# Two transformer layers in one kernel: the order of attention products over TensorE's row groups, and the key sums of the last queries

## The chip, the cores and the metric

The kernel runs on one core of one Trainium2 chip. The metric is the device time of one execution, in microseconds: the median of several runs. A profile of one further execution gives the engines' instructions with their starts and lengths. The profile calls the engines PE (TensorE's products) and PEld (its weight loads), DVE (VectorE), ACT (ScalarE), POOL (GpSimd) and SP (which issues DMAs).

## The reference

Two layers work on x of shape (2, 2048, 256), 16 heads. Each layer normalises x and adds the product of two branches, `x + s * g`.

```python
xn = _layernorm(x)
s = _L0_attn_ref(xn, ...)            # linear attention
g = _silu(_L0_ffn_ref(xn, ...))      # a transformer block: causal softmax attention
x = x + s * g                        #   with 16 channels a head, then 8 experts, top 2
xn = _layernorm(x)
s = _L1_attn_ref(xn, ...)            # causal softmax attention, real and imaginary parts,
g = _silu(_L1_ffn_ref(xn, ...))      #   together 32 channels a head; int4 weights, LoRA
x = x + s * g
```

What matters here are the two causal softmax attentions, each over 2048 queries and keys, 2 batches and 16 heads:

```python
scores = jnp.where(causal, q @ k.T * scale, -big)
probs = jax.nn.softmax(scores, -1)
out = probs @ v
```

## The kernel before

**Three parts.** Attention 1 (of the first layer's block, with the linear attention, the norms and the routing dealt in between), the experts, and attention 2 (with the second layer's other branch in between). Both attentions are built by one function, `run_attention` (L550), which runs over 2 batches x 4 groups of four heads. The four heads of a group lie on partitions 0 to 31, 32 to 63, 64 to 95 and 96 to 127, so each head's products use one row group of TensorE's array, 32 rows high and 128 columns wide, and products of four heads can stand in the array side by side. This is called the row shape below. The products of weights with values use the column shape (128 rows, 32 columns a head), and everything else the whole array.

**Two passes.** Pass A (`pass_a`, L568) takes 128 queries against up to 512 keys and forms scores (L575), with queries on the partitions; DVE takes their maximum (L594), which is later subtracted from the queries. In attention 1 a diagonal piece gets the causal mask by four small bf16 products a head, of 128, 96, 64 and 32 columns (`hide`, L529, product at L534); in attention 2 DVE adds the mask and takes the maximum (L588). Pass B (`pass_b`, L601) takes 256 queries against a pair of key tiles with keys on the partitions: two products of 256 columns a head (L609; on the diagonal one of 256 and one of 128), in attention 2 one or two three-row bf16 products that bring in the maximum (`less_maximum`, L1691, products at L1697, L1698 and L1700), and on the diagonal four mask products (`hide_pair`, L536, product at L541). ACT then takes the exponential (L621) into `pt`. One turn `u` of the loop in `run_attention` makes a **unit**: pass A for one piece and pass B for one pair, four heads each.

**Banks.** Scores go to PSUM, which is eight banks of 512 fp32 columns a partition. Pass A takes two neighbouring banks for two heads, since one DVE instruction reduces both; pass B takes one bank a head. A full unit thus takes two pairs and four single banks, all eight.

**Sums of the weights.** In attention 2 POOL adds the weights `pt` over the key tiles of two pairs into `ps` (L1717, L1721, L1722), and a product with ones sums `ps` over the partitions (L1751); the products with values are L1740. For the last 256 queries of the last group, POOL leaves out the last pairs (`direct`, L1725: `p >= c - 1`, c = 7) and products of `pt` itself with ones give the sums (L1747).

**What orders the work.** Nothing is issued as the functions run: each calls `S = plan.step`, which notes a step with its strand (S for scores and sums, A and B for the passes' DVE and ACT work, prep, lin, mix, gate, end and others), engine, cost, reads, writes, and for TensorE where it stands (`on`: a row group's number, "col" or "all"). A planner (`Plan.run` and `Plan.advance`, L223) then searches for the order, with a beam and random handicaps, under a model of time that has queues, banks and buffers; within one strand and engine the order of the calls is kept. Steps of the strands prep, lin, mix and gate may not come before `plan.pace`. In the model before, a product in row shape begins when its group is free and the queue behind it goes on 0.01 us later, whatever group comes next:

```python
if t > groups[s.on] or st.cold[s.on]:
    t += s.load
...
done, free["PE"] = t + s.cost + self.TAIL - self.GAP, sent + 0.01
```

A step on TensorE is one product of pass A, or both products of pass B, or all four masks of a head, or the maximum's products of a head. In a unit their order is, with A0 for pass A of head 0 and so on: A0, B2, A1, B3, the masks and late maxima of these four, then A2, B0, A3, B1 and theirs.

Of the kernel before, what the change touches and what calls it, by code (L numbers as in the profile page):

```python
# [17 lines left out]
P = 128  # L18
# [76 lines left out]
class State:  # L95


    def __init__(self, plan):
        self.main = next(iter(plan.queues.get(("S", "PE"), ())), None)
        self.can = {k: q[0] for k, q in plan.queues.items() if not q[0].before}  # L100
        self.waits = [s.before + (s is not plan.queues[s.key][0]) for s in plan.steps]
        self.ready = [0.0] * len(plan.steps)
        self.slot = [None] * len(plan.bufs)
        self.left = [b.uses for b in plan.bufs]
        self.until = [0.0] * len(plan.bufs)
        self.guest = [None] * len(plan.bufs)
        self.since = {k: [0.0] * (plan.BANKS if k == "s" else len(x)) for k, x in plan.kinds.items()}
        self.free, self.groups, self.cold = {}, [0.0] * 4, [True] * 4
        self.mode, self.used, self.held = None, 0.0, {}
        self.todo, self.done, self.value = len(plan.steps), [], 0.0  # L110
# [10 lines left out]
class Plan:  # L121
# [101 lines left out]
    def advance(self, st, handicaps, until):  # L223

        free, groups, can, ready = st.free, st.groups, st.can, st.ready
        while st.todo:
# [4 lines left out]
            for key, s in can.items():  # L231
# [6 lines left out]
                if eng == "PE":  # L238
                    closed = strand != "S" and not (gap and st.used + s.cost <= self.LIMIT)
                    x = top if s.kind != st.mode else groups[s.on] if s.row else top - self.MODE  # L240
                    if x > busy:
                        busy = x
# [43 lines left out]
            if s.eng == "PE":  # L286
                st.used = st.used + s.cost if key[0] != "S" else 0.0
                kind = s.kind
                if kind != st.mode:
                    if kind == "row":  # L290
                        groups[:] = [max(t, x) for x in groups]
                    st.cold[:] = [True] * 4
                if s.row:
                    if t > groups[s.on] or st.cold[s.on]:
                        t += s.load
                    st.cold[s.on] = False
                elif t > max(groups) or st.cold[0]:
                    t += s.load
                    st.cold[0] = False
                done, free["PE"] = t + s.cost + self.TAIL - self.GAP, sent + 0.01  # L300
                if kind == "row":
                    st.mode, groups[s.on] = "row", t + s.cost
                    worth /= 4
                else:
                    st.mode, groups[:] = s.on, [t + s.cost] * 4
            elif s.eng == "SP":
                free["SP"] = t + 0.06
# [70 lines left out]
def kernel(ctx: ExitStack, tc: tile.TileContext, i: dict, out: bass.AP):  # L378
# [81 lines left out]
    def t_row(n):  # L460
        return 0.00167 * n
# [65 lines left out]
    T_HIDE_A, T_HIDE_B = 0.15, 0.28  # L527

    def hide(out, j, mask):  # L529

        r = slice(32 * j, 32 * j + 32)
        for q in range(4):
            cols = slice(32 * q, P)
            nc.tensor.matmul(out[:, cols], ident_h[r, q], mask[r, q, cols], start=False, stop=q == 3)  # L534

    def hide_pair(out, j, mask):  # L536

        r, v = slice(32 * j, 32 * j + 32), out.rearrange("p (n k) -> p n k", n=2)
        for q in (3, 2, 1, 0):
            cols = slice(0, 32 * q + 32)  # L540
            nc.tensor.matmul(v[:, :, cols], ident_h[r, q], mask[r, q, :, cols], start=False, stop=q == 0)  # L541
# [8 lines left out]
    def run_attention(plan, make, prepare, subtract, sum_keys, finish, last_sum, before=None, others=(), between=False, causal=None):  # L550
# [17 lines left out]
        def pass_a(g, t, k, i, w, mx, parts):  # L568
# [11 lines left out]
            def products(x):  # L580
                return S("S", "PE", t_row(w), lambda: score(x), r=[(g.qt, t), *((g.kt, n) for n in keys)], w=[(s, x)], on=i + x)

            def rest():
                for x in range(2) if diagonal and causal is None else ():
                    S("S", "PE", T_HIDE_A, lambda x=x: hide(s.t[:, x, w - P : w], i + x, mask_q), r=[(s, x), "ident_h", "mask_q"], w=[(s, x)], on=i + x)
# [15 lines left out]
        def pass_b(g, c, p, j, pt):  # L601
# [5 lines left out]
            def score():  # L607
                for n, (kj, q0, at) in enumerate(halves_of(c, p)):
                    nc.tensor.matmul(  # L609
                        s.t[:, at], g.kt.t[r, kj * P : (kj + 1) * P], g.qt.t[r, QC * c + q0 : QC * (c + 1)],  # L610
                        start=n == 0 and not ahead, stop=n == 1 and not (diagonal or before and not ahead),
                    )

            def rest():
                if before and not ahead:
                    S("S", "PE", 0.25 * t_row(w), before(g, c, j, s, diagonal, False, not diagonal), r=[s, g.mh[c]], w=[s], on=j, load=0.026)
                if diagonal:
                    S("S", "PE", T_HIDE_B, lambda: hide_pair(s.t[:, : 2 * P], j, mask_h), r=[s, "mask_h"], w=[s], on=j)
# [4 lines left out]
            reads = [(g.kt, 2 * p), (g.kt, 2 * p + 1), (g.qt, 2 * c), (g.qt, 2 * c + 1)]  # L623
            opener = None
            if ahead:
                opener = S("S", "PE", 0.25 * t_row(w), before(g, c, j, s, diagonal, True, False), r=[g.mh[c]], w=[s], on=j, load=0.026)
                reads.append(s)
            step = S("S", "PE", t_row(w), score, r=reads, w=[s], on=j)
            return opener or step, rest, weigh
# [4 lines left out]
        for u in range(at + last_sum + 1):  # L634
# [10 lines left out]
            first = None  # L645
            for i in (0, 2):


                more = []
                if a:  # L650
                    products, after_a = pass_a(g, t, k, i, wa, mx, parts)
                for x in range(2):
                    if a:
                        plan.pace = products(x)
                        first = first or plan.pace
                    if b:
                        step, rest, weigh = pass_b(gb, cb, p, (i + 2 + x) % 4, pt)
                        first = first or step
                        more.append((rest, weigh))
                if a:  # L660
                    after_a()
                for rest, _ in more:
                    rest()
                for _, weigh in more:
                    weigh()
# [848 lines left out]
    with ExitStack() as sc:  # L1514
# [176 lines left out]
        def less_maximum(G, c, j, s, diagonal, first, last):  # L1691
            r = slice(32 * j, 32 * j + 3)

            def product():
                m = G.mh[c].t[r]
                if diagonal:
                    nc.tensor.matmul(s.t[:, :P], ones_h[r], m[:, P:], start=first, stop=False)  # L1697
                    nc.tensor.matmul(s.t[:, P : P + QC], ones_h[r], m, start=False, stop=last)  # L1698
                else:
                    nc.tensor.matmul(  # L1700
                        s.t.rearrange("p (n q) -> p n q", n=2), ones_h[r], m[:, None].to_broadcast([3, 2, QC]),
                        start=first, stop=last,
                    )

            return product

        def sum_keys(G, c, pair, last):
# [17 lines left out]
            direct = G.b == B - 1 and G.g == NG - 1 and c == NT // 2 - 1 and p >= c - 1  # L1725
# [156 lines left out]
```

## Time and profile before

| | |
|---|---|
| median of 3 runs | 3334.01 us (3331.4 to 3335.59) |
| the profiled execution | 3333.86 us, its span 3332.1 us, granted TensorE clock 0.982 |
| PE, DVE, ACT, POOL busy | 96%, 64%, 49%, 49% of the span |
| attention 1, experts, attention 2 | 0 to 1374, 1374 to 1909, 1909 to 3332 us |
| L575, products of pass A | 5120 passes, 1282.3 us busy |
| L609, products of pass B | 9216 passes, 1239.8 us busy |
| L621, exponential on ACT | 2304 of 577 ns mean |
| L594, maximum on DVE | 1024 of 1122 ns mean |

An fp32 product shows as two passes, each with a weight load of its own, so 5120 passes are 2560 products. Busy time of PE is the time in which at least one product is in the array; products of different row groups lie over each other in it. Some records of products are missing from a trace. The timeline of an engine gives start, length, line, tiles, shapes and count, and merges neighbours of one line and shape, which then show with the length of all together; idle time and what ended it stand in brackets.

### The profile page before, as it was taken

Reading aid. Unit: us, or ns where it says so; the run is one execution under the profiler, and the core shown is the slowest. Engines: PE = TensorE matmul, PEld = TensorE weight load, DVE = VectorE, ACT = ScalarE, POOL = GpSimd, SP = SyncE. Lnnn points to the kernel's source line nnn. Section 1 sums busy time; section 2 is a strip of 40 time slices with the busy share of each in tenths; the row PEclk is TensorE's granted clock in tenths of the full one; section 3 lists DMA queues with packets and bytes.
Section 4 is the critical chain, followed back from the end, with each engine's and each line's share of the span. In section 5 each row is a group of like instructions: output and inputs, shape, how many; then the busy total and the mean of one; then the engine's idle time right before and its main releaser. Section 6 shows DMA issues by size and latency. Waiting matters only on the chain.

```text
span 3332.1 us, 92022 instructions
## 1 busy us (share of the span) xinstructions
PE 3205.3 (96%) x39748; PEld 2271.7 (68%) x39748; DVE 2132.9 (64%) x4250; ACT 1623.4 (49%) x3264; POOL 1620.8 (49%) x2006
## 2 busy tenths in 40 slices
PE   7999999989999999979999989999999999999998
PEld 5677777767777776656666646666766666767775
DVE  5677677667777767641112057787777776777785
ACT  3565555555555555511112155555554555544554
POOL 5442222333233222310000057898987776878887
PEclk9999999999999999989999989999999999999999
DMA  5000000000000010133342131110101001000000
GB/s 198 2 2 2 5 8 8 17 30 26 6 11 5 9 45 13 49 109 115 109 131 94 64 105 43 38 43 29 39 17 33 27 17 40 23 12 23 14 29 24
DMA packets 99742, 134.51 MB, mean 40 GB/s; under 512 B 9461, under 2 KB 76739, under 8 KB 99334
## 3 DMA queue, kind: packets, MB, share of 16 engines
q1 hardware_dynamic: 93190, 114.74, 10.6%
q0 software_dynamic: 6144, 13.88, 1.3%
q8 instruction: 311, 5.10, 0.6%
q14 instruction: 97, 0.79, 0.1%
HBM read 93.75 MB, written 37.75 MB: 39 GB/s over the span
## 4 chain that ended last, share of the span: by engine, by line
PE 50%; DVE 3%; POOL 2%; ACT 1%; issue 1%; DMA 0%; POOLq 0%; another core or an unknown queue 0%; SPq 0%; DVEq 0%; ACTq 0%
PE banks L575 9%; PE banks L609 8%; PE banks L414 8%; PE banks L1740 7%; PE s L1488 7%; PE s L1494 7%; PE banks L1751 2%; PE banks L1700 1%; PE banks L541 1%; PE banks L1698 1%; DVE mx L594 1%; POOL ps L1721 1%; ACT pt L621 1%; POOL ps L1717 0%; POOL ps L1722 0%
## 5 line engine op out<-in xcount | busy, mean ns | idle before, releaser
L621 ACT ACTIVATE pt<-banks 128x512 f32<-128x512 f32 (+1 forms) x2304 | 1160.7, 577 | 721.9 <-PE banks L609 321.3
L594 DVE TENSOR_REDUCE mx<-banks 128x2 f32<-128x1024 f32 (+3 forms) x1024 | 1119.1, 1122 | 337.4 <-PE banks L609 141.7
L575 PE MATMUL banks<-carried,carried 32*128 32x512 f32 (+3 forms) x5120 | 1282.3, 566 | 25.0 <-DVE mx L594 10.5
L609 PE MATMUL banks<-carried,carried 32*128 32x256 f32 (+1 forms) x9216 | 1239.8, 378 | 3.8 <-issue 3.7
L609 PEld LDWEIGHTS banks<-carried,carried 32*128 32x128 f32 x9216 | 972.1, 186 | 42.8 <-issue 15.8
L575 PEld LDWEIGHTS banks<-carried,carried 32*128 32x128 f32 x5120 | 545.3, 185 | 242.3 <-issue 108.6
L1717 POOL TENSOR_TENSOR ps<-pt 128x1024 f32<-128x1024 f32 (+1 forms) x159 | 346.7, 2181 | 113.8 <-ACT pt L621 101.8
L1721 POOL TENSOR_TENSOR ps<-ps,pt 128x1024 f32<-128x1024 f32 x127 | 302.4, 2381 | 69.3 <-ACT pt L621 64.8
L848 POOL TENSOR_TENSOR ra<-raw,rope 128x128 f32<-128x128 f32 x128 | 60.1, 470 | 566.3 <-ACT raw L860 496.1
L1700 PE MATMUL banks<-mh,ones_h 3*128 3x512 bf16 x896 | 272.0, 382 | 7.5 <-ACT mh L1688 3.5
L1722 POOL TENSOR_TENSOR ps<-ps,pt 128x1024 f32<-128x1024 f32 (+1 forms) x127 | 269.1, 2119 | 10.0
L911 PE MATMUL banks<-pt,vt 128*32 128x256 f32 (+1 forms) x4608 | 269.1, 371 | 4.3 <-DVE mx L594 3.0
L1740 PE MATMUL banks<-pt,vt 128*32 128x256 f32 (+1 forms) x4608 | 269.0, 371 | 2.5 <-ACT pt L621 2.5
L1497 DVE TENSOR_TENSOR ye<-s,b 128x256 f32<-128x256 f32 x64 | 27.2, 424 | 380.6 <-PE s L1494 380.6
L588 DVE CUSTOM_DVE_ANT_0 banks<-banks,causal 128x384 f32<-128x384 f32 (+3 forms) x512 | 240.3, 515 | 40.5 <-PE banks L575 25.2
L1489 ACT ACTIVATE hm<-s,b1c 128x512 f32<-128x512 f32 x128 | 87.8, 687 | 347.2 <-PE s L1488 346.0
L1488 PE MATMUL s<-xt,carried 128*128 128x512 f32 x512 | 228.2, 604 | 9.7 <-DVE xt L1421 9.7
L1494 PE MATMUL s<-carried,hm 128*128 128x256 f32 x1024 | 223.6, 379 | 0.0
L1740 PEld LDWEIGHTS banks<-pt,vt 128*32 128x32 f32 x4608 | 135.2, 110 | 129.5 <-ACT pt L621 26.4
L1494 PEld LDWEIGHTS s<-carried,hm 128*128 128x128 f32 x1024 | 194.6, 190 | 33.3 <-issue 7.7
L911 PEld LDWEIGHTS banks<-pt,vt 128*32 128x32 f32 x4608 | 134.0, 109 | 114.4 <-issue 15.7
L1488 PEld LDWEIGHTS s<-xt,carried 128*128 128x128 f32 x512 | 97.4, 193 | 131.2 <-issue 110.2
(276 smaller groups left out, 4166.9 us busy)
## 6 DMA issues: line engine op xcount, KB each, us to landing
carried<-in_L_ffn_W_dram SPq DMA_DIRECT2D x32, 1024.0 KB
gl<-g_dram SPq DMA_DIRECT2D x64, 256.0 KB
slots_in<-zero SPq DMA_DIRECT2D x8, 1024.0 KB
slots_out<-ye SPq DMA_DIRECT2D x16, 512.0 KB
xe<-slots_in SPq DMA_DIRECT2D x15, 512.0 KB
s_dram<-lo SPq DMA_DIRECT2D x16, 256.0 KB
hn<-in_L_attn_x_dram SPq DMA_DIRECT2D x16, 256.0 KB
g_dram<-gs SPq DMA_DIRECT2D x16, 256.0 KB
```

What stands on the lines that cost most here:

```text
L575: nc.tensor.matmul(s.t[:, x, :w], g.qt.t[r, t * P : (t + 1) * P], g.kt.t[r, 512 * k : 512 * k + w], start=True, stop=not (diagonal and cau ...
L594: S("A", "DVE", t_dve(2 * w), lambda: nc.vector.tensor_reduce(mx.t[:, t % 2, i : i + 2, k], s.t[:, :, :w], AX.X, ALU.max), r=[(s, 0), (s, ...
L609: nc.tensor.matmul(s.t[:, at], g.kt.t[r, kj * P : (kj + 1) * P], g.qt.t[r, QC * c + q0 : QC * (c + 1)], start=n == 0 and not ahead, stop=n ...
L621: S("B", "ACT", t_act(w), lambda: nc.scalar.activation(pt.t[:, j, :w], s.t[:, :w], AF.Exp, scale=0.25), r=[s], w=[(pt, j)])
L911: nc.tensor.matmul(av.t[32 * j : 32 * j + 32, q0:QC], vts[G.vn][:, kj, j], pt.t[:, j, at], start=n == 0, stop=n == len(tiles) - 1,)
L1488: nc.tensor.matmul(ps, w1[:, k, f * P : (f + 1) * P], xt[:, k], start=k == 0, stop=k == 1)
L1494: nc.tensor.matmul(ps[:, :D], hm[:, f, s * P : (s + 1) * P], w2[:, f], start=f == 0, stop=f == FF // P - 1)
L1700: nc.tensor.matmul(s.t.rearrange("p (n q) -> p n q", n=2), ones_h[r], m[:, None].to_broadcast([3, 2, QC]), start=first, stop=last,)
L1717: nc.gpsimd.tensor_tensor(ps.t[:, :, q0:], pt.t[:, :, same], pt.t[:, :, odd], ALU.add)
L1721: nc.gpsimd.tensor_tensor(ps.t, ps.t, pt.t[:, :, even], ALU.add)
L1722: nc.gpsimd.tensor_tensor(ps.t[:, :, q0:], ps.t[:, :, q0:], pt.t[:, :, odd], ALU.add)
L1740: nc.tensor.matmul(av.t[32 * j : 32 * j + 32, q0:QC], G.vt.t[:, kj, j], pt.t[:, j, at], start=n == 0, stop=False)
```

## The change

The planner's model is changed: a product in row shape is sent only when the product before it in its group has begun, and what stands behind it in TensorE's queue waits with it. A change of shape waits until all groups are done.

```diff
+                    if s.row and s.kind == st.mode and began[s.on] > t:
+                        t = busy = began[s.on]
...
+                if s.kind != st.mode:
+                    sent = max(sent, max(groups) + self.MODE)
+                    st.mode, groups[:], began[:] = s.kind, [sent] * 4, [sent] * 4
                 if s.row:
-                    if t > groups[s.on] or st.cold[s.on]:
-                        t += s.load
-                    st.cold[s.on] = False
...
+                    t = max(groups[s.on], sent + s.load)
+                    began[s.on], groups[s.on] = t, t + s.cost
                     worth /= 4
                 else:
-                    st.mode, groups[:] = s.on, [t + s.cost] * 4
+                    t = max(groups[0], sent + s.load)
+                    began[:], groups[:] = [t] * 4, [t + s.cost] * 4
+                done, free["PE"] = t + s.cost + self.TAIL - self.GAP, sent + 0.007
```

Each single product is a step of its own: `hide`, `hide_pair` and `less_maximum` return lists of products with their costs, and `hide` and `hide_pair` now give the narrowest mask first. In attention 1 (`before` is None) the steps of a unit are dealt out: each group's products stand in their order, and the four lists are merged by the time at which the product ahead in the group would begin. In attention 2 they are sorted by half and phase, which is the order of before.

```diff
-                        step, rest, weigh = pass_b(gb, cb, p, (i + 2 + x) % 4, pt)
...
+            order = []
+            for j, q in enumerate(queues):
+                began, until = -1.0, 0.0
+                for n, entry in enumerate(q):
+                    order.append((began, j, n, entry))
+                    began, until = until, until + entry[0]
+            order.sort(key=lambda x: x[:3])
+            if before:
+                order = [(0, j, 0, entry) for _, j, entry in sorted(by_step, key=lambda x: x[0])]
+            for _, j, _, (cost, fn, r, w_, load, *_) in order:
+                step = S("S", "PE", cost, fn, r=r, w=w_, on=j, load=load)
+                first = first or step
+            if a:
+                plan.pace = step
```

`plan.pace` is now the last row product of a unit, where it was the last product of pass A. Last, the sums of the last 256 queries of the last group are all made by products with ones, none by POOL:

```diff
-            direct = G.b == B - 1 and G.g == NG - 1 and c == NT // 2 - 1 and p >= c - 1
+            direct = G.b == B - 1 and G.g == NG - 1 and c == NT // 2 - 1
```

The instructions themselves stay the same in number and size, but for 48 more products with ones of `pt` and 12 fewer of `ps`, and nine fewer adds on POOL; the order on every engine is planned anew. Line numbers shift by up to 16: pass A's product stays L575, pass B's is L610, the masks are L527 and L537, the maximum's products L1711, L1719 and L1720, the products with values L1756, and those with ones L1767 and L1763.

## The prediction

> **What bounds the kernel now.** I read the shares of the engines first, then the three parts of the program as windows, then TensorE's own timeline inside one unit of attention, and the end last.
>
> ```profile
> PE 3205.3 (96%) x39748; PEld 2271.7 (68%) x39748; DVE 2132.9 (64%) x4250; ACT 1623.4 (49%) x3264; POOL 1620.8 (49%) x2006
> ...
> 0.00:1374.00 1374.00, 1324.47 (x16740) 978.94 (x16740) 971.94 (x1811) 764.58 (x1628) 450.27 (x1086) 0.99 0.07 24
> 1374.00:1909.00 535.00, 506.04 (x2142) 337.80 (x2141) 108.42 (x325) 124.51 (x197) 35.56 (x57) 0.97 0.32 103
> 1909.00:3332.00 1423.00, 1374.77 (x20870) 955.00 (x20868) 1052.52 (x2115) 734.27 (x1440) 1134.99 (x863) 0.98 0.11 32
> ```
>
> The columns of the last three are the window, its length, busy PE, PEld, DVE, ACT and POOL, the granted clock, DMA. TensorE carries both attentions (first and third window: 1324 of 1374 and 1375 of 1423 us) at a clock of 0.98 to 0.99, so time is gained where TensorE's work packs more tightly. Busy does not mean packed; the timeline of TensorE tells that (start, length, line, tiles, shape, count):
>
> ```profile
> 603.44 1.14 PE L575 MATMUL banks<-carried,carried 32*128 32x512 f32 x8
> 604.51 0.75 PE L911 MATMUL banks<-pt,vt 128*32 128x256 f32 x12
> ```
>
> Four row products of 512 columns, one a row group, stand here together and nothing blocks them. Each runs as two passes whose starts lie 427 ns apart, so a product of N fp32 columns takes N/600 us, 853 ns here. The next shape starts 1.07 us after, so a row stretch costs **853 + 217 ns**. 217 ns is the price of a change to row shape; the same count gives 157 ns for column stretches and 157 to 217 ns for whole-array ones. Now a full unit of attention 1, where each group owes two products (1707 ns):
>
> ```profile
> 594.37 0.69 PE L575 MATMUL banks<-carried,carried 32*128 32x512 f32 x1
> ...
> 595.35 0.47 PE L609 MATMUL banks<-carried,carried 32*128 32x256 f32 x1
> 595.37 0.67 PE L575 MATMUL banks<-carried,carried 32*128 32x512 f32 x1
> ...
> 596.40 0.33 PE L421 MATMUL banks<-cst,x 128*128 128x128 f32 x1
> ```
>
> 2.03 us, 324 over 1707. In the middle some passes last 0.47 and 0.67 where others last 0.37 and 0.59: their weights were not loaded ahead, because the product stood in the program behind one whose group was still occupied. That is the other 107 ns. A diagonal unit is worse:
>
> ```profile
> 598.95 0.69 PE L575 MATMUL banks<-carried,carried 32*128 32x512 f32 x1
> ...
> 599.91 0.23 PE L534 MATMUL banks<-mask_q,ident_h 32*128 32x128 bf16 x2
> ...
> 600.14 0.48 PE L609 MATMUL banks<-carried,carried 32*128 32x256 f32 x1
> ...
> 600.22 0.69 PE L575 MATMUL banks<-carried,carried 32*128 32x512 f32 x2
> ...
> 601.58 0.42 PE L911 MATMUL banks<-pt,vt 128*32 128x256 f32 x4
> ```
>
> 1924 ns of work took 2630. The second half (600.14 on, all with exposed loads) starts behind the masks of the first.
>
> **The change, part by part.** I cut TensorE's program, before and after, into stretches of one shape, and laid those of before on the trace. "Work" is the busiest group's sum of products.
>
> *1. Attention 1, dealing.* Before: 338 row stretches, work 503.8 us. By form, (shortest measured time − work − 217 ns) x count: 125 full units 0.107 = 13 us; 20 of work 1434, 0.433 = 9; 19 of 1924, 0.487 = 9; 23 of 1770, 0.115 = 3; 14 of 1221, 0.38 = 5; all forms together **75 us** lost to order. Dealt, a full unit goes A0 A1 B2 B3 B0 B1, the second halves of B2 and B3, A2 A3, the second halves of B0 and B1. Each product stands behind one that is running, so loads go ahead: by hand, starts 7 ns apart, first pass 107 ns late, then 1829 to 1836 ns and 91 ns to the next shape, 1927 instead of 2031. I leave a tenth of the 75 in the other forms: **−68 us** (bounds −75 and, if the diagonal forms keep half, −45).
>
> *2. Attention 1, cutting up.* Products are steps of their own now, and in the new program the planner splits some 30 full units in two: 31 stretches of work 1280 and 25 of 853 (together 2133, not 1707). Work of row stretches is 519.6 us, +15.8; there are 343 instead of 338 (5 x 0.217 = 1.1) and 258 whole-array stretches instead of 228 (30 x 0.19 = 5.7). **+22.5 us.** This is counted, not estimated.
>
> *3. Attention 1, banks.* A unit needs all eight PSUM banks. Before, its start needs four (A0 A1, B2, B3), B0 0.55 us later, A2 A3 and B1 near 0.97. Dealt, six are needed within 30 ns. What covers a late bank is that B0 only holds up the second halves of B2 and B3, due at 0.53 us. I took each bank's last reader from the trace of ACT and DVE: over 240 full units, with the old starts and banks, B0 or B1 would come more than that cover late 212 times, **81 us** in sum; with the banks given out anew at the same starts, all waits are 43 us. The old order's own, counted alike, are 36. So the growth lies between +7 and +45. DVE and ACT bound nothing on average (a unit has 2 x 1.12 of DVE and 4 x 0.58 of ACT against some 4 of PE), and the planner knows of banks, but filling work between units is the same as before (a quarter under 1.5 us): **+22**. A planner that finds better starts could make it less than nothing; I hold −15 for that.
>
> The Trainium skill ("TensorEngine Tiling (Array Packing)", Performance Considerations, PSUM Bottleneck) speaks against the change: tiling speeds up TensorE but not the emptying of PSUM, which may become the limit. The rows agree in part (36 us of late banks now); were the rule the whole story, parts 1 and 3 would cancel, and the sum would be +22 for attention 1 instead of −24.
>
> *4. Attention 2.* Within a unit the sorted order is the old one, so forms can be looked up: 228 of 236 new row stretches occur in the trace of before. Their shortest overheads, and the nearest forms for the other 8, sum to 179.3 us (252 before: 182.8), **−3.5**. Row work falls 544.8 to 542.1, **−2.7**; 14 column stretches fewer, x 0.157, **−2.2**. Masks (L541) now go smallest first: in the trace the next group's product is let in when the third of four masks has begun, which comes 27 + 53 instead of 107 + 80 ns after the first. 107 ns earlier, of which some 85 show, in 64 diagonal units: **−5.4** (0 to −10).
>
> *5. The end.*
>
> ```profile
> 3304.29 0.64 PE L1751 MATMUL banks<-ps,ones 128*32 128x256 f32 x8 [1.02 <-POOL ps L1722]
> ...
> 3311.94 0.64 PE L1751 MATMUL banks<-ps,ones 128*32 128x256 f32 x8 [2.18 <-POOL ps L1722]
> ...
> 3319.18 0.64 PE L1751 MATMUL banks<-ps,ones 128*32 128x256 f32 x8 [1.20 <-POOL ps L1722]
> ...
> 3321.15 1.70 PE L1747 MATMUL banks<-pt,ones 128*32 128x256 f32 x32
> ```
>
> The brackets are TensorE's waits for POOL's sums: 4.4 us. Nine POOL adds of 2.4 us go; three L1751 groups (0.43 to the next start) become three L1747 groups (1.56). Column work rises 3.8 in all. ACT (8 x 2.3 us of weights against 27 busy us of PE between 3290 and 3323) does not come last in their place, the products themselves do. **−4.4 + 3.8 = −0.6** (−4.4 to +3.8).
>
> *6. The rest.* The strands that are paced (prep, lin, mix, gate, with their loads on SP) hang on a unit's last row product instead of its last A product, under 1 us later in queues that are filled a unit ahead: nothing, and at most a few us if a group's start is late. The experts (1374 to 1909) are untouched. A new plan also shifts every other wait; attention 2's row stretches hold 38 us of waits and its column stretches 27, and I allow ±15 without a sign.
>
> Sum: −68 + 22.5 + 22 − 3.5 − 2.7 − 2.2 − 5.4 − 0.6 = **−38 us**. The profiled execution took 3333.86 (span 3332.1), the median of the runs is 3334.01, so the sum carries over: 3334 − 38 = **3296 us**.
>
> **Rivals.** *Banks eat it:* starts stay where they are (+45 instead of +22) and a third of the diagonal forms' loss remains (+15): −38 + 38 = 0, **3334**. For it: fill between units is unchanged. Against: banks can be given out anew. *Slower, by banks at the start of a unit:* a shorter unit ends earlier but its weights leave ACT no earlier, so each unit's shortfall grows by the 0.1 to 0.45 us gained, say 0.2 x 240 = 48, on top of the 45: −38 − 22 + 93 = +33, **3367**. It decides from 0.25 us of added stall a unit (60 us without part 3, over 240). Against: 2.5 us of other work lie between units on average. *All of the gain:* the better model finds starts without new waits (part 3 at −15, −37 against my sum): **3259**. *Nothing is dealt:* excluded for attention 1, where the program shows dealt forms; in attention 2 it is so already, and is in the sum.
>
> **How the numbers follow.** Forecast (a gain, 3268 to 3326): 0.60. All of the gain: 0.12. Banks eat it: 0.14. Slower: 0.14. Faster by over 0.2% (under 3327, about the least that a measurement here can tell from none) takes the first two and a little of the third: 0.74; within 0.2%: 0.11; slower: 0.15. The range takes both ends of part 3, the ±15 and a little of the rivals: **3264 to 3338**.
>
> **What would show it.** Full units of attention 1 at 1.93 us between starts of shapes; diagonal ones of 1924 near 2.2; more waits of L575 and of the weight loads of L610 for ACT and DVE at units' starts; the first window shorter by some 24 us, the third by some 12 to 15; no wait of TensorE for POOL after the last 256 queries begin. I am wrong if the first window is not shorter: then banks, not order, set its units.

## The result, and the profile after

The changed kernel is **slower**: 3420.9 us (median of four runs, 3418.1 to 3424.3) against 3334.8, ratio 1.026 with an interval of 1.0242 to 1.0278. I had forecast 3296 and a range up to 3338. Its profiled execution took 3418.8 us. The page's shares and the three parts, cut at the same places as before (columns as in the prediction's first fence):

```profile
PE 3248.5 (95%) x39820; PEld 2217.2 (65%) x39820; DVE 2136.0 (63%) x4250; ACT 1622.2 (47%) x3264; POOL 1593.9 (47%) x1997
...
0.00:1449.00 1449.00, 1355.93 (x16901) 922.06 (x16901) 977.62 (x1825) 770.85 (x1643) 447.99 (x1086) 0.99 0.07 23
1449.00:1983.00 534.00, 497.79 (x1979) 330.06 (x1979) 102.34 (x311) 117.29 (x182) 35.36 (x57) 0.96 0.32 103
1983.00:3417.00 1434.00, 1394.75 (x20944) 965.05 (x20942) 1056.04 (x2115) 734.09 (x1440) 1110.60 (x854) 0.98 0.11 32
```

The clock is the same, the experts are the same. The first window grew by 75 us, the third by 11, although TensorE has nearly the same products (72 passes more) and its weight loads are busy 54 us less, as a tighter packing should have it. From here on I cut at the experts' first product and after their last (the expert line's first and last start, one row for each kernel; before first, then after):

```profile
L1488 PE MATMUL s<-xt,carried x512: 592/592/1222, 1446.2 to 1903.1; 128*128 128x512 f32 x171
```
```profile
L1504 PE MATMUL s<-xt,carried x512: 592/592/1221, 1521.0 to 1977.5; 128*128 128x512 f32 x171
```

Attention 1 by this cut: 1446.2 and 1521.0, **+74.8**. Attention 2, from the last number to the span's end: 1429.0 and 1439.5, **+10.5**.

What its queues waited for in attention 1 has changed. Weight loads only; the columns are total us, times, longest; before and then after:

```profile
PEld banks L575 <- DVE mx L594: 28.8, 67, 3.4
PEld banks L911 <- ACT pt L621: 13.1, 42, 0.4
PEld banks L841 <- ACT pt L621: 11.2, 34, 0.4
```
```profile
PEld banks L575 <- DVE mx L596: 35.7, 70, 3.2
PEld banks L927 <- ACT pt L635: 29.9, 59, 3.3
PEld banks L857 <- ACT pt L635: 25.6, 39, 2.1
PEld banks L575 <- ACT pt L635: 19.8, 42, 1.6
```

Over all lines, of products and loads, waits for ACT's exponentials went from 45 to 155 us, those for DVE's maxima from 59 to 77 (a wait of a load may lie beside a running product, so these are not all lost time). Of the 155 us only 36 stand at products of the units themselves (L575 and L610; 2 before); the other 120 or so stand at the products that follow a unit (44 before). The two largest of these wait for banks and not for `pt`: L857 does not read `pt`, and 57 of the 59 waits of L927 end with an exponential of a later unit than the one whose `pt` the product reads. The engine that is waited for is itself busy only 53% of the first window. Its row says what for (attention 1; busy us, mean ns, idle time before it and its releasers; before, then after):

```profile
L621 ACT ACTIVATE pt<-banks 128x512 f32<-128x512 f32 (+1 forms) x1152 | 583.5, 576 | 347.1 <-PE banks L609 197.9 <-PE banks L541 84.3 <-issue 42.3
```
```profile
L635 ACT ACTIVATE pt<-banks 128x512 f32<-128x512 f32 (+1 forms) x1152 | 580.0, 576 | 437.8 <-PE banks L610 254.2 <-PE banks L537 74.9 <-PE banks L575 54.8
```

The exponentials take as long as before. They start later: ACT waits 56 us longer for pass B's products. TensorE waits for ACT, and ACT waits for TensorE. One unit and the start of the next show how (TensorE's timeline; start, length, line, shape, count; the rows of ACT after it):

```profile
146.94 0.70 PE L575 MATMUL banks<-carried,carried 32*128 32x512 f32 x2
146.95 0.70 PE L610 MATMUL banks<-carried,carried 32*128 32x256 f32 x4
...
147.49 0.79 PE L610 MATMUL banks<-carried,carried 32*128 32x256 f32 x6
147.92 0.59 PE L575 MATMUL banks<-carried,carried 32*128 32x512 f32 x2
148.12 0.60 PE L610 MATMUL banks<-carried,carried 32*128 32x256 f32 x4
...
149.26 0.92 PE L857 MATMUL banks<-wqkv,ht 128*128 128x192 f32 x4 [0.32 <-ACT pt L635]
150.11 0.70 PE L575 MATMUL banks<-carried,carried 32*128 32x512 f32 x2
150.12 0.81 PE L610 MATMUL banks<-carried,carried 32*128 32x256 f32 x4
...
150.95 0.72 PE L610 MATMUL banks<-carried,carried 32*128 32x256 f32 x8
151.48 0.59 PE L575 MATMUL banks<-carried,carried 32*128 32x512 f32 x2
```
```profile
148.61 2.07 ACT L635 ACTIVATE pt<-banks 128x512 f32<-128x512 f32 x4 [2.58 <-PE banks L610]
```

The first unit is packed as I had worked out. A2 and A3 begin at 147.92, 0.98 us after its start, so B2 and B3 are through groups 2 and 3 by about then. But ACT begins on B2 only at 148.61, 1.67 us after the start, and had nothing else to do. In the unit of before that the prediction shows (start 594.37) it begins after 1.25 us:

```profile
595.62 1.58 ACT L621 ACTIVATE pt<-banks 128x512 f32<-128x512 f32 x3 [0.56 <-PE banks L609]
```

148.61 is just after the end of the first products of B0 and B1 (second passes from 148.12, a pass takes 0.37 to 0.38). The trace's semaphore events say why. The products' counts all go to one semaphore, and they appear there in the order of the program. By its record B2's second product ended at 148.08, but its count was posted at 148.54, 0.04 us after the first products of B0 and B1 had ended (148.49 and 148.50), and ACT began 0.07 us later. In the dealt order those two stand ahead of B2's second product in the program. The full units agree: in the median ACT begins 0.12 us after the first products of B0 and B1, which is 0.54 us after B2's own second product; before, it began 0.12 us after B2's second product.

ACT then needs 2.07 us for four weights. The next whole-array product finds no bank and waits 0.32 us. In the next unit B0 and B1 have to wait: their weight loads come at 150.73 and 150.94, each after an instruction of ACT (PEld's timeline; the row holds both):

```profile
150.73 0.54 PEld L610 LDWEIGHTS banks<-carried,carried 32*128 32x128 f32 x8 [0.20 <-ACT pt L635]
```

They hold up the second halves of B2 and B3 behind them (150.95, 0.84 us after the start, where the first unit has 0.55), and with them A2 and A3 (1.37 instead of 0.98).

Over all full units the medians, counted from a unit's start, are:

| full units of attention 1 | ACT begins on B2 | B2, B3, B0, B1 are empty | A0 A1, A2 A3 are empty | time over the 1707 of work, median |
|---|---|---|---|---|
| before | 1.25 us | 1.85, 2.34, 2.83, 3.32 | 2.46, 3.59 | 324 ns |
| after | 1.68 | 2.28, 2.77, 3.26, 3.75 | 2.40, 3.56 | 626 ns |

So the banks of B0 and B1 are due 0.5 and 0.9 us earlier (0.03 after the start instead of 0.55 and 0.97), and all four of pass B are given back 0.4 us later. A unit thus holds 21.9 bank-microseconds where it held 19.0: each bank from when its product is due in an unhindered unit until it is empty, A2 and A3 due near 0.97 in both. Spread over eight banks that is 0.36 us a unit if banks set the pace; over some 200 units, by estimate, about 70 us.

Which of the two waits costs more, that of the next shape's first product or that of B0 and B1 inside a unit, can be read from the 93 full units of after that stand in one stretch (126 before), if a pass of N columns is taken to end N/1200 us after it starts. In the median the twelve products end 137 ns over the work, as I had worked out (before: 233). It is the next shape's first product that comes late. With a bank at hand it stands 91 ns behind them; in the median it comes 429 ns behind, 2.33 us after the unit's start and 0.05 us after ACT has emptied B2's bank (2.28). It is more than 40 ns late after 75 of the 93 units, 30 us in sum; before, after 3 of 126, 2 us. What the units take inside beyond those 137 ns, the waits of B0 and B1 and of what stands behind them, comes to 20 us; before, beyond its 233 ns, to 17 us.

The accounts of attention 1 by stretches of one shape (from a stretch's first product to that of the next shape, the last one up to the experts' first product):

| | before | after | difference |
|---|---|---|---|
| row stretches, work of the busiest group | 503.8 | 519.6 | +15.8 |
| row stretches, time over the work | 198.3 | 235.5 | +37.2 |
| whole-array stretches (228, then 258) | 472.3 | 492.0 | +19.7 |
| column stretches | 262.1 | 264.1 | +2.0 |

### The profile page after: what moved, and what is told of

Its sections match the earlier page's. It is cut to its first block, busy times and chain, and to the rows that moved or that the text cites. A ratio compares the mean times of both kernels' runs of the same rounds, so it can differ in the third digit from the quotient of the medians.

```text
span 3417.0 us, 92182 instructions
## 1 busy us (share of the span) xinstructions
PE 3248.5 (95%) x39820; PEld 2217.2 (65%) x39820; DVE 2136.0 (63%) x4250; ACT 1622.2 (47%) x3264; POOL 1593.9 (47%) x1997
## 4 chain that ended last, share of the span: by engine, by line
PE 83%; DVE 7%; ACT 3%; POOL 3%; issue 2%; DMA 0%; another core or an unknown queue 0%; SPq 0%; DVEq 0%; POOLq 0%; ACTq 0%
PE banks L575 17%; PE banks L610 15%; PE banks L409 7%; PE banks L927 7%; PE s L1504 7%; PE s L1510 6%; PE banks L1756 6%; DVE mx L596 3%; ACT pt L635 3%; PE banks L857 2%; PE banks L537 2%; PE banks L1189 2%; PE banks L1767 2%; PE banks L416 2%; PE banks L1711 1%
## 5 line engine op out<-in xcount | busy, mean ns | idle before, releaser
L575 PE MATMUL banks<-carried,carried 32*128 32x512 f32 (+3 forms) x5120 | 1273.1, 562 | 35.0 <-DVE mx L596 14.1
L610 PE MATMUL banks<-carried,carried 32*128 32x256 f32 (+1 forms) x9216 | 1216.3, 379 | 1.8 <-ACT pt L635 0.9
L610 PEld LDWEIGHTS banks<-carried,carried 32*128 32x128 f32 x9216 | 916.2, 187 | 76.7 <-issue 26.0
L575 PEld LDWEIGHTS banks<-carried,carried 32*128 32x128 f32 x5120 | 531.9, 185 | 256.0 <-issue 113.2
L1733 POOL TENSOR_TENSOR ps<-pt 128x1024 f32<-128x1024 f32 (+1 forms) x156 | 337.6, 2164 | 103.6 <-ACT pt L635 89.2
L1737 POOL TENSOR_TENSOR ps<-ps,pt 128x1024 f32<-128x1024 f32 x124 | 294.3, 2374 | 66.2 <-ACT pt L635 61.9
L1711 PE MATMUL banks<-mh,ones_h 3*128 3x512 bf16 x896 | 275.8, 383 | 5.7 <-DVE carried L1658 2.0
L927 PE MATMUL banks<-pt,vt 128*32 128x256 f32 (+1 forms) x4608 | 271.3, 373 | 6.5 <-ACT pt L635 6.2
L1756 PE MATMUL banks<-pt,vt 128*32 128x256 f32 (+1 forms) x4608 | 270.7, 373 | 2.3 <-ACT pt L635 2.1
L1738 POOL TENSOR_TENSOR ps<-ps,pt 128x1024 f32<-128x1024 f32 (+1 forms) x124 | 261.1, 2106 | 9.7
L1756 PEld LDWEIGHTS banks<-pt,vt 128*32 128x32 f32 x4608 | 135.8, 110 | 132.1 <-ACT pt L635 32.0
L927 PEld LDWEIGHTS banks<-pt,vt 128*32 128x32 f32 x4608 | 134.8, 110 | 130.4 <-ACT pt L635 29.9
```

The lines of the kernel that those rows point to most:

```text
L575: nc.tensor.matmul(s.t[:, x, :w], g.qt.t[r, t * P : (t + 1) * P], g.kt.t[r, 512 * k : 512 * k + w], start=True, stop=not (diagonal and cau ...
L610: nc.tensor.matmul(s.t[:, at], g.kt.t[r, kj * P : (kj + 1) * P], g.qt.t[r, QC * c + q0 : QC * (c + 1)], start=n == 0 and not ahead, stop=n ...
L927: nc.tensor.matmul(av.t[32 * j : 32 * j + 32, q0:QC], vts[G.vn][:, kj, j], pt.t[:, j, at], start=n == 0, stop=n == len(tiles) - 1,)
L1711: nc.tensor.matmul(s.t.rearrange("p (n q) -> p n q", n=2), ones_h[r], G.mh[c].t[r][:, None].to_broadcast([3, 2, QC]), start=first, stop=last,)
L1733: nc.gpsimd.tensor_tensor(ps.t[:, :, q0:], pt.t[:, :, same], pt.t[:, :, odd], ALU.add)
L1737: nc.gpsimd.tensor_tensor(ps.t, ps.t, pt.t[:, :, even], ALU.add)
```

## The experiments

Theories: **late banks** (the dealt order makes pass B's banks the limit), against **the cutting up** (more pieces, counted in the program), **the new model** (it plans units at worse places) and **a wrong picture of TensorE** (dealt products pack worse than I reckoned). The median of before differs from chip to chip, so ratios are to before on the same chip.

| label | attention 1, us | attention 2 | ratio [95% interval] |
|---|---|---|---|
| before | 1446.2 | 1429.0 | 1 |
| after | 1521.0 | 1439.5 | 1.026 [1.0242, 1.0278] |
| e1_old_order | 1447.3 | 1438.9 | 1.0055 [1.0039, 1.0072] |
| e2_late_banks | 1439.4 | 1436.9 | 1.0037 [1.0022, 1.0052] |
| e3_model_alone | 1447.2 | 1436.8 | 1.0045 [1.0028, 1.0062] |
| e4_dealt_old_model | 1529.7 | 1432.6 | 1.0292 [1.0275, 1.0309] |
| e5_after_short_emptying | 1440.3 | 1439.3 | 1.0044 [1.0028, 1.0059] |
| e6_before_short_emptying | 1424.2 | 1427.1 | 0.995 [0.9928, 0.9972] |
| e7_direct_alone | 1443.4 | 1433.1 | 0.9977 [0.9963, 0.9991] |
| e8_by_own_start | 1434.3 | 1431.9 | 0.9975 [0.9961, 0.999] |
| e9_own_start_direct | 1438.0 | 1439.2 | 0.9954 [0.994, 0.9968] |
| e10_own_start_old_model | 1439.9 | 1437.1 | 0.9953 [0.9939, 0.9966] |
| e11_tie_turned | 1438.1 | 1416.7 | 1.0101 [1.0084, 1.0118] |

Before's median is 3334.8 us beside after, 3330.1 beside e1 to e4 and 3336.1 beside e5 to e8. The last three rows' times are from chips that differ more (3354.4 beside e9 and e10, 3286.1 beside e11); there only the ratios compare. e6, whose attention 2 has the program of before, shows 1427.1 against 1429.0, and e8's is 1431.9: some 3 us of a part is no difference.

**e1_old_order.** The changed kernel, with attention 1 sorted as attention 2 is, and pass A's masks behind the products of their half, as before; model, single steps and the sums as changed.

```diff
-                        by_step += [((i, 0, 2 * x), i + x, e) for e in products(x)]
+                        by_step += [((i, 0, 2 * x) if e[4] is None else (i, 1, x - 2), i + x, e) for e in products(x)]
...
-            if before:
+            if True:
                 order = [(0, j, 0, entry) for _, j, entry in sorted(by_step, key=lambda x: x[0])]
```

> The changed kernel, but attention 1's units sorted as attention 2's are (the order of before); single products as steps, the new model and the sums with ones stay. Theory banks (dealing asks for six of eight PSUM banks at a unit's start and leaves the second pair of pass A the last ones, which come late): attention 1 falls back to 1446 us or a little under, from 1521; in all 3330 to 3350 us. Rival model (the new model or the single steps make worse plans whatever the order within a unit): attention 1 stays over 1490, in all over 3390. Rival cutting-up (the split units' own price, 22 us): in all about 3398, unless the splits stay.

All but 1 of the 75 us go: the order makes them. The model and the single steps cost attention 1 nothing. Of the 10.6 us that its profiled execution is longer than before's, 9.9 stand in attention 2; the ratio says 0.55%, some 18 us, and where the rest is stays open.

**e2_late_banks.** The changed kernel, with each half of a unit dealt by itself: A0 A1 B2 B3, the second halves of B2 and B3, A2 A3 B0 B1, the second halves of B0 and B1.

```diff
-                    order.append((began, j, n, entry))
+                    if i != half:
+                        began, until, half = -1.0, 0.0, i
+                    order.append(((i, began, kind), j, n, entry))
```

> The changed kernel, but attention 1's units are dealt by halves: A0 A1 B2 B3, the second halves of B2 and B3, and only then A2 A3 B0 B1 and the second halves of B0 and B1, so that the four banks of the second half are asked for 0.5 us after the start, while each product still stands behind one that runs. Theory banks: most of the 75 us comes back and some of the 68 us that order costs is gained as well; attention 1 at 1390 to 1450 us, in all 3285 to 3345. Rival model: over 3390. Rival exposed loads do not matter (dealing gains nothing even without late banks): attention 1 at 1446 or more, in all 3340 or more.

Products are dealt as before, one behind the other in each group, and attention 1 is 82 us shorter than after's and 7 shorter than before's (the whole is still 0.37% over before, with 8 us more in attention 2). So it isn't dealing as such. ACT begins on B2 after 1.31 us here. Two things are changed at once, though: B0 and B1 need their banks later, and B2 and B3 are finished first. e11 keeps most of the first as it is in the changed kernel and has the second.

**e3_model_alone** is the kernel before with nothing but the new model; **e4_dealt_old_model** is the changed kernel with the old one. The core of the edit, for e3 (for e4 it is turned round):

```diff
-                    if t > groups[s.on] or st.cold[s.on]:
-                        t += s.load
+                    t = max(groups[s.on], sent + s.load)
```

> The kernel before with the planner's new model alone; steps, order within a unit and sums as before. Theory banks: the order within a unit is the old one, so 3320 to 3350 us. Rival model: 3380 to 3420.

> The changed kernel with the planner's old model: dealt units, single steps, sums with ones. Theory banks: as slow as the changed kernel or slower, 3400 to 3440 us, since the order within a unit is what asks for banks. Rival model: 3300 to 3350.

In attention 1 the model alone moves 1 us, and with the dealt order it saves 9 of 84. In attention 2 it costs 8 us (1436.8 against 1429.0); the steps, masks and sums without it cost 4, near the spread of 3.

**e5_after_short_emptying, e6_before_short_emptying.** In both kernels, attention 1 only, ACT and DVE read at most 128 columns of each bank; TensorE's program stays the same, instruction by instruction. The weights that ACT no longer writes are constants, so part of attention 1 is left out, the same part in both. The line of ACT in the edit (DVE's is alike):

```diff
-nc.scalar.activation(pt.t[:, j, :w], s.t[:, :w], AF.Exp, scale=0.25)
+nc.scalar.activation(pt.t[:, j, : P if before is None else w], s.t[:, : P if before is None else w], AF.Exp, scale=0.25)
```

> The changed kernel with the emptying of PSUM made cheaper in attention 1, and TensorE's program the same instruction for instruction: the exponential on ACT reads and writes 128 columns instead of 512 or 384, the maximum on DVE reads 128 columns instead of up to 512 (so part of attention 1 is left out; the weights left over stand at 1). Theory banks: with banks free early the dealt units cost what was worked out for them, 1.93 us for a full one, and attention 1 is some 45 us shorter than that of the old order with the same cut (the next run): about 1355 us against 1400. Rival order (the dealt program itself is slower, whatever the banks): over 30 us longer than the old order's.

> The kernel before with the same cut of ACT's and DVE's work in attention 1, its control (the same part is left out). Theory banks: only the 36 us of late banks and a few other waits go; the 75 us that order costs stay: attention 1 at 1390 to 1415 us, and longer than the dealt one's. Rival order: shorter than the dealt one's by over 30 us.

After's attention 1 falls by 80.7 us, before's by 22.0. The difference between the two orders shrinks from 74.8 to 16.1: **59 of the 75 us go when the banks are emptied sooner**, with TensorE's program left alone. The 16 that stay are 6.9 in row stretches (15.8 of work more from the cutting up, 8.9 less over the work), 4.8 in whole-array and 4.3 in column stretches. Neither theory's number was met: the first had the dealt order well ahead of the other here. Full units go from 626 to 306 ns over their work, 245 at best, where I had worked out 220. Late banks are not gone, though: TensorE's waits for exponentials and maxima fall from 232 to 117 us, against 63 in e6. What the dealt order would be worth with no late bank at all, no run shows. The waits of loads that were shown for after, in e5:

```profile
PEld banks L575 <- DVE mx L596: 19.8, 47, 2.6
PEld banks L930 <- ACT pts L635: 16.5, 40, 2.4
PEld banks L860 <- ACT pts L635: 14.5, 29, 1.8
```

ACT still begins on B2 1.68 us after a unit's start in e5, although half of these waits are gone. So that lateness comes from TensorE's order of products and not from what the banks do; long emptying makes it cost more. It still costs here: the product behind a full unit is more than 40 ns late after 53 of 93, 11 us in sum.

**e7_direct_alone.** The kernel before, with the line for the last sums alone.

```diff
-            direct = G.b == B - 1 and G.g == NG - 1 and c == NT // 2 - 1 and p >= c - 1
+            direct = G.b == B - 1 and G.g == NG - 1 and c == NT // 2 - 1
```

> The kernel before with the sums of the last 256 queries by products with ones alone; nothing else. Worked out before as -4.4 + 3.8 us: within 5 us of the kernel before either way, attention 1 unchanged, no wait of TensorE for POOL after the last 256 queries begin. Rival (it carries the 10 us that attention 2 lost): 8 to 12 us slower.

A gain of 0.23%, 8 us (3 to 12). Its profiled execution, 3335.7 us, does not show it: TensorE's products of `ps` wait 0.9 us for POOL instead of 5.4, as meant, and attention 2 is no shorter. Where the 8 us are won stays open.

**e8_by_own_start.** The kernel before in everything but attention 1, which has single products, the new model and another sort: by the time at which a product itself would begin, and not the one ahead of it.

```diff
-                    order.append((began, j, n, entry))
+                    order.append((round(until, 4), entry[4] is not None, -n, j, n, entry))
```

> Attention 2 as before; in attention 1 single products as steps, the new model, and each product put where it would itself begin, not where the one ahead of it begins: a bank is asked for as late as the group's work allows, and masks of one head no longer hold up the other heads. Theory banks: keeps most of what halves gave (7 us in attention 1) and adds the diagonal units, some 20 us of order of which late banks may eat half: attention 1 at 1415 to 1440, in all 3300 to 3330. Rival (late banks take all that order gives): attention 1 at 1440 to 1455, in all 3325 to 3345.

A full unit gets the order of e2. Attention 1 is 11.9 us shorter than before's, the whole is 0.25% faster: most of my 68 us do not appear even so, but the sign is right. Full units take 279 ns over their work (324 before), ACT begins on B2 after 1.31 us, and waits for banks come to 116 us, near before's 104.

**e9_own_start_direct, e10_own_start_old_model.** e8 with the line of e7; and this with the model of before (`PlanDealt(` to `Plan(`).

> e8_by_own_start plus the changed line for the sums of the last 256 queries. Where the two gains add, as they should if each stands in its own part of the program: 9.5 + 8.1 us under the kernel before, ratio 0.9947, near 3318; attention 1 near 1434, attention 2 near 1430. Rival: the 8 us of the sums' line alone were a difference of plans, since its profiled execution showed none of it; then the ratio stays at 0.9975 or above, 3327 or more.

> e9_own_start_direct with the planner's model of before in attention 1, so that only the single products and their order by own expected start are new there. If the order of the program makes the gain of e8_by_own_start in attention 1 (12 us: 1446.2 to 1434.3), it stays: attention 1 at 1431 to 1438, the ratio within 0.15% of that of e9. If the new model makes it, by placing units where banks are free, attention 1 goes back to 1443 to 1450 and the ratio rises by about 0.0035. The model moved attention 1 by 1 us without the order (1447.2) and by 9 with the dealt order (1529.7 against 1521.0), so I hold the first, with up to 5 us for the model.

The gains add (0.9954; the product of the two is 0.9952), and the model gives nothing (0.9953). **The faster version** is thus e9 or e10, 0.46% under before and 3% under the changed kernel.

**e11_tie_turned.** The changed kernel with one tie of its sort turned: groups 2 and 3 first.

```diff
-            order.sort(key=lambda x: x[:3])
+            order.sort(key=lambda x: (x[0], x[1] < 2, *x[1:3]))
```

> The changed kernel with one tie of its sort turned round: where two products of a unit fall on the same time, those of groups 2 and 3 stand first. A full unit then goes B2 B3 A0 A1, the second halves of B2 and B3, B0 B1, A2 A3, the second halves of B0 and B1: six products still need their banks within 0.45 us of the start, but B2 and B3 are finished before B0 and B1 begin, so that ACT can empty them as early as before (in the changed kernel it begins on B2 1.76 us after the unit's start, in the kernel before 1.36). The planner cuts up less here: by the count of row work and stretches attention 1 would be some 16 us shorter than 1521.0 from that alone. Theory 'banks are given back late': attention 1 falls by far more, to 1437 to 1460, and ACT begins on B2 at 1.3 to 1.4 us. Rival 'banks are taken early' (B0 and B1 at the start, as my prediction had it): most of the loss stays, attention 1 at 1490 to 1510. Whole time 3335 to 3360 by the first, 3390 to 3410 by the second.

(The 1.76 and 1.36 us of that text weigh units with masks more heavily; counted once a unit, in full units, they are 1.68 and 1.25.) 1.0101 instead of 1.026: 1.6 of the 2.6% are gone, and the rest is partly attention 2's, as e1 shows. There is no trace of before on this chip. If every part scales as the whole does (3334.8 / 3286.1), attention 1 is 1459, so by this estimate some 60 of the 75 us are gone, of which some 16 by less cutting up. The whole, 3368 us on that scale, lies between the two expectations and nearer the first. A full unit and its first exponentials:

```profile
254.42 0.48 PE L610 MATMUL banks<-carried,carried 32*128 32x256 f32 x2
...
254.74 0.60 PE L610 MATMUL banks<-carried,carried 32*128 32x256 f32 x4
254.96 0.59 PE L575 MATMUL banks<-carried,carried 32*128 32x512 f32 x2
255.17 0.38 PE L610 MATMUL banks<-carried,carried 32*128 32x256 f32 x2
255.38 0.59 PE L575 MATMUL banks<-carried,carried 32*128 32x512 f32 x2
...
256.37 1.98 PE L1189 MATMUL banks<-wqkv,lx 128*128 128x512 f32 x4
```
```profile
255.72 2.06 ACT L635 ACTIVATE pt<-banks 128x512 f32<-128x512 f32 x4 [1.95 <-issue]
```

The same twelve products, the same groups; ACT begins 1.30 us after the start instead of 1.67 (median of full units 1.29), and the unit is over after 1.95 (median 1.97). B0 and B1 are still due early (by my estimate from the order, some 0.45 us after the start), but nothing that could run sooner stands behind them: a late B0 now holds up A2 and A3 alone, whose groups are occupied for another half microsecond. The earlier signal to ACT and the milder hold-up come from one swap, but in full units the trace parts them: the product behind the unit is more than 40 ns late after 18 of 83 units, 3 us in sum where it was 30, and the waits inside come to 13 us where they were 20. In full units the earlier signal is thus the larger share; for the other units the shares are not parted.

## Why the prediction was wrong, point by point

*1. Dealing, −68.* The packing is right in units that find their banks: the dealt stretches of 1280 and 853 take 209 and 205 ns over their work, diagonal units of the form that the prediction shows go from 2.63 us (median) to 2.29 in spite of late banks, and full units, for which I had 220, take 259 (227 at best) in e11 and 306 (245 at best) in e5. As a sum it was earned nowhere: in the changed kernel the time over the work rose by 37 us over all row stretches, and with short emptying it is 173 us against the old order's 182, with waits for banks left in both.

*2. Cutting up, +22.5.* The counts were right. The 30 more whole-array stretches took 19.7 us instead of 5.7, but not by their price. That price, the change of shape, was about right: the median stretch takes 0.21 us over its products before and 0.22 after. Over all of them but the last this time rose by 18.3 us, 12 of them idle time inside the stretches, and with short emptying (e5 against e6) by 2.6 alone; 3.3 us stand in the last stretch, which runs into the experts. So the excess is mostly late banks, which I had looked for in the row stretches only, and belongs to part 3.

*3. Banks, +22, bounds +7 to +45.* **This step failed.** Parts 1 and 3 and five changes of shape were to give −45 in the row stretches; they gave +37. Had part 1 been earned whole, part 3 would be 37 + 68 − 1 = +104 there. The step "took each bank's last reader from the trace of ACT and DVE", with "the old starts and banks", so it moved the takers of the banks and left the givers where they were. In the changed kernel ACT begins on B2 0.43 us later, because its wait counts B0 and B1, which now stand ahead of B2's second half. And the step looked for late banks only at B0 and B1, inside the unit. In full units the larger part stands behind the unit, where I had no term: B2's bank is empty at 2.28 us instead of 1.85, the unit's products were to end near 1.83, and until then all eight banks are taken (30 us in 93 units, against 20 inside them). Inside, the step counted B0's and B1's lateness once; in the queue it goes on to the second halves of B2 and B3, and from them to A2 and A3. The bound was no bound: it held one side fixed that the change moves.

I had weighed the Trainium skill's rule on this ("TensorEngine Tiling (Array Packing)", Performance Considerations, PSUM Bottleneck) and let my own count of the rows overrule it. The runs side with it: 59 of the 75 us vanish when emptying is shortened and TensorE's program is left alone.

*4. Attention 2, −13.8.* Wrong in sign: +10.5. The row work fell by 2.7 as counted. But the row stretches' time over it rose by 11.5 us (221.0 to 232.5), where looking up shortest overheads had given a fall. If stretches are told apart only by the products that they hold, the shortest measured overheads did fall, by 3 us; the waits beyond them grew by 15. The new model alone costs 8 of it (e3), for units with the old products; I had not priced it, and only allowed ±15 without a sign. By which waits it loses them stays open.

*5. The end, −0.6.* Waits for POOL went as said: the last products with ones stand without one (three more groups of 32 than before, and 1.72 to 1.84 us to the next start where I went by 1.56):

```profile
3389.17 1.91 PE L1763 MATMUL banks<-pt,ones 128*32 128x256 f32 x32
3396.60 1.91 PE L1763 MATMUL banks<-pt,ones 128*32 128x256 f32 x32
3403.73 1.91 PE L1763 MATMUL banks<-pt,ones 128*32 128x256 f32 x32
```

Measured alone the line gains 8 us (3 to 12), where my bound was 4.4.

*6. The rest, 0.* The experts took 456.5 us against 456.9. Nothing else was seen.

*Rivals.* "Slower, by banks at the start of a unit" had the sign, at +33 and a chance of 0.14; measured were +86. It sought the stall at a unit's start, and in full units the larger part stands at its end. Its reason, that the weights "leave ACT no earlier", was still too kind; they leave later. My closing test ("I am wrong if the first window is not shorter: then banks, not order, set its units") decided rightly, but for the "not order": it is the order that sets when the banks come back.

## What to carry to other kernels

When an order is changed, ask of each result not only when its product ends but which products its reader's wait counts: where products are counted in program order, as here, a reader goes on only when everything ahead of its product in the program is done. Ask also what stands behind a unit that takes all the banks: it waits for the first bank given back. Deal products out so that each bank's last product comes as soon as it can, depth first within a bank (e8, e2, e11), and (argued here, not tested by itself) take a new bank only when nothing due sooner stands behind it; a bare tie in a sort was worth 1.6%. A cost that is worked out from old waits and old release times is a bound only if the change cannot move either.

## What the runs showed of the hardware that I had not expected

A product in row shape whose bank is late holds up products of other, free groups behind it, in program order: in the unit at 150.11, B0 and B1 held the second halves of B2 and B3 by 0.29 us and A2 and A3 by 0.39. A product's count can be posted long after the product has ended: B2's second product ended at 148.08 and was counted at 148.54, after products that began later but stand ahead of it in the program. And an engine that is 47% busy over the span (ACT) can be the one waited for 155 us of 1521, since its work comes in bursts of four exponentials, 2.07 us, behind one signal.
